# Two graph layers on one core: a block's projections dealt out between tiles of sums, and the second layer's sums zeroed by a product

## The chip, the cores and the metric

The kernel runs on one core of a Trainium2 chip. The metric is the device time of one execution in microseconds, as a median of repeated runs; lower is better. The engines are named as the profile names them: PE multiplies matrices (PEld loads its stationary operand), DVE is the vector engine, ACT the scalar engine, POOL issues the gathers and SP issues most other transfers.

## What is computed

There are N = 6250 nodes with D = 256 features, E = 100000 edges sorted by their target, and R = 8 kinds of edges. The input is normalised, goes through two graph layers, is added to the input, is normalised again, and goes through a mixture of 8 experts that picks 2 for each node. The two layers are this, cut to what matters:

```python
def _rgcn_conv(x, W, Wroot, b, src, dst, etype):
    xs = x[src]
    seg = dst * R + etype
    sums = segment_sum(xs, seg, num_segments=N * R)
    cnt = segment_sum(ones, seg, num_segments=N * R)
    mean = (sums / maximum(cnt, 1.0)[:, None]).reshape(N, R, -1)
    return x @ Wroot + b + einsum('nrd,rde->ne', mean, W)

h = relu(_rgcn_conv(layernorm(x), W1, Wroot1, b1, src, dst, etype))
h = _rgcn_conv(h, W2, Wroot2, b2, src, dst, etype)
x = x + h
x = x + moe(layernorm(x))
```

The targets are denser at low node numbers, so the first blocks of nodes have many more edges than the last.

## The kernel before, in words

**Preparation** (up to the first gather, at 83.5 us) normalises x, writes it to memory as three bfloat16 pieces (`xs[0]`), and works out where each tile of edges lands.

**A layer** is `layer(k)`, k = 0 and 1. The edges are 782 tiles of 128. A *group* is 1 to 6 neighbouring tiles; there are 194 groups, and `seq` is their order, which takes groups from the front (few nodes, many edges) and from the end (many nodes, few edges) in turn. One pass of the loop over `q` is a *step* and serves one group.

- `tiles_in(g)` takes one of two accumulators `pg` (PSUM, one bank of 2 KB for each of the 2 halves of the features, and a third in the first layer for the counts), has ACT fill it with zeros (L672), and for each tile has POOL gather 128 source rows into one of 13 buffers `ge` (L680) and DVE make the 0/1 matrix `oh` (L686). It is called one step ahead.
- `sums(g)` multiplies: 6 products on PE for each tile (L696; 3 pieces by 2 halves), and in the first layer a seventh with ones for the counts (L699). They accumulate in `pg`. The last product that reads a `ge` buffer sets that buffer free for a later gather.
- `add(g)` has DVE add `pg` to a ring in SBUF (L710). There are two rings, one for each end of the nodes; each holds RB = 3 blocks of 128 nodes.

**A block** is 128 nodes; there are 49. `whole[b]` is the step after which no edge of block b is left. The block's work is then due at fixed steps after it:

- `counts` and `invert` bring the counts to the partitions (first layer only);
- `project` (two steps on) multiplies the block's sums by the weights: 18 products in fp32 (2 halves for the root and 8 relations), each executed as two passes on PE, 36 passes in all (L783). They are made in five *pairs* of relations through a small PSUM tile `pr` with two buffers, and DVE adds each relation into `h` (L791, L793);
- `clear` (two steps on) has ACT zero the block's place in the ring (L800), after the projections have read it;
- `finish` (two steps on) writes the block's result: the three pieces of the next layer's input, or the output and its normalisation;
- `turn` (three steps on) transposes it, and `logits` (four on) makes the expert scores in the second layer.

The step in the loop, in order: `tiles_in` of the next group, `project` and `clear`, `turn`, `finish`, `sums`, `invert` and `logits`, `add`, then `root`, `counts` and `join`. This is the order of the program. A scheduler in the compiler's front end then orders each engine's instructions by that and by when it takes their operands to be ready, so products of `project` and of `sums` can already be mixed on PE. [...]

**Bounds.** `_plan` also works out which part of a ring a group may touch at each step (`bounds`, checked at run time), so that an `add` need not wait for the projections that read other blocks. READ is the number of steps after `whole[b]` at which no add may touch block b any more, TAKE = 3 the number after which the block's cleared place may be used again.

**After the layers** 53 tiles of 256 chosen rows go through the experts (L1186 to L1230).

Of the kernel before, what the change touches and what calls it, by code (L numbers as in the profile page):

```python
# [39 lines left out]
BF16 = mybir.dt.bfloat16  # L40
# [8 lines left out]
P = 128  # L49
# [45 lines left out]
Z = 4.8  # L95
WIN = 64
RB = 3
READ = 2
TAKE = 3
EARLY = 30  # L100

# [1 line left out]
def _plan(N, E, R):  # L103

    T = -(-E // P)

    def windows(ts, n):

        mid = n // 2
        lo, hi = [0] * n, [-(1 << 30)] * n
        for t in ts:
            for k in range(n + 1):
                i0, i1 = t * P, max(0, t + k - mid) * P
                mean = N * (i1 * i1 - i0 * i0) / (E * E)
                sd = 2 * N * i0 / (E * E) * math.sqrt(abs(i1 - i0)) + 0.004 * abs(mean)
                if k < n:
                    lo[k] = min(lo[k] if t != ts[0] else 1 << 30, math.floor(mean - Z * sd) - (k < mid))
                if k:  # L120
                    hi[k - 1] = max(hi[k - 1], math.ceil(mean + Z * sd) + (1 if k <= mid else 2))
        shift = -min(lo)
        w = [(a + shift, b + shift) for a, b in zip(lo, hi)]
        return shift, w, max(b for _, b in w)


    NB = -(-N // P)
    mid = max(0, round((N / 4 - P / 2) / P))
    split = round(T * math.sqrt((mid + 0.5) * P / N))
    regions = []  # L130
    t = 0
    while t < T:
        left = (split if t < split else T) - t
        for n in range(min(6, left), 0, -1):
            ng = max(1, min(36, left) // n)
            shift, w, width = windows((t + n // 2, t + n * (ng - 1) + n // 2), n)
            if width <= WIN:
                break
        regions.append((t, n, ng, shift, w, width))
        t += n * ng  # L140
    groups = []
    for r, (t0, n, ng, *_) in enumerate(regions):
        for g in range(ng):
            groups.append((t0 + g * n, n, r))
    NG = len(groups)
    up = [g for g in range(NG) if groups[g][0] < split]
    down = list(range(NG - 1, len(up) - 1, -1))
    size = [sum(groups[g][1] for g in s) for s in (up, down)]
    seq, at, n = [], [0, 0], [0, 0]
    while len(seq) < NG:  # L150

        s = int(n[1] * (size[0] - EARLY) < n[0] * size[1])
        if at[s] == len((up, down)[s]):
            s = 1 - s
        g = (up, down)[s][at[s]]
        seq.append(g)
        at[s] += 1
        n[s] += groups[g][1]
    step = {g: q for q, g in enumerate(seq)}

    whole = []
    for b in range(NB):
        if b == mid:
            whole.append(NG - 1)
            continue
        p = math.sqrt((b + 1 if b < mid else b) * P / N)
        dev = Z * math.sqrt(E * p * (1 - p)) + 1
        t = int(min(E - 1, E * p + dev) // P) if b < mid else int((E * p - dev) // P)
        whole.append(step[next(g for g, (t0, n, _) in enumerate(groups) if t0 + n > t)])


    bounds = []
    for g in range(NG):
        read, taken = ([b for b in range(NB) if whole[b] + n < step[g]] for n in (READ - 1, TAKE))
        if g < len(up):
            bounds.append((sum(b < mid for b in read) or -NB, sum(b < mid for b in taken) + RB))
        else:
            n = sum(b > mid for b in read)
            bounds.append((NB - sum(b > mid for b in taken) - RB, NB - n if n else 2 * NB))
    return T, regions, groups, seq, len(up), mid, whole, bounds  # L180
# [3 lines left out]
def kernel(  # L184
# [20 lines left out]
    nc = tc.nc  # L205
    N, D = x.shape
    E = src.shape[0]
# [428 lines left out]
    with tc.If(go == 1) as cmp:  # L636
        with ExitStack() as arm:
# [4 lines left out]
            hTs = ap.tile([P, NB, KD, P], F32, name="hTs", bufs=1)  # L642
            zeros = ap.tile([P, WIN], F32, name="zeros", bufs=1)
            nc.vector.memset(zeros, 0.0)
            rings = [ap.tile([P, KD + 1, R, RING + WIN], F32, name=f"ring{i}", bufs=1) for i in range(2)]

            step = {g: q for q, g in enumerate(seq)}
# [8 lines left out]
            def layer(k):  # L656
# [11 lines left out]
                def tiles_in(g):  # L668
                    t0, n, r = groups[g]
                    pg = psum.tile([P, nd, R, WIN], F32, name="pg", tag="pg", bufs=2)  # L670
                    wd = regions[r][5]
                    state["zeroed"] = nc.scalar.copy(pg[:, :nd, :, :wd],  # L672
                                                     zeros[:, None, None, :wd].to_broadcast([P, nd, R, wd]))
                    got = []
                    ohs = ap.tile([P, OHW], BF16, name="oh", bufs=3)
                    o0 = 0
                    for t in range(t0, t0 + n):
                        m = P if t < EC else ER
                        ge = ap.tile([P, 3, KD, P], BF16, name="ge", bufs=13)
                        nc.gpsimd.indirect_dma_start(  # L680
                            out=ge[:m].rearrange("p s k d -> p (s k d)"), out_offset=None, in_=xs[k][:, :],
                            in_offset=bass.IndirectOffsetOnAxis(ap=idx[:m, t : t + 1], axis=0))
                        a, b = regions[r][4][t - t0]
                        oh = ohs[:m, o0 : o0 + (b - a) * R].rearrange("p (r d) -> p r d", r=R)
                        o0 += (b - a) * R
                        nc.vector.tensor_scalar(oh, iota16[:m].rearrange("p (r d) -> p r d", r=R)[:, :, a:b],  # L686
                                                rel[:m, t : t + 1], None, op0=OP.is_equal)
                        got.append((ge, oh, m, a, b))
                    state[g] = (pg, got)

                def sums(g):
                    pg, got = state[g]
                    for ge, oh, m, a, b in got:
                        for c in range(KD):
                            for s in range(3):
                                nc.tensor.matmul(pg[:, c, :, a:b], ge[:m, s, c, :], oh, start=False, stop=False,  # L696
                                                 skip_group_check=True)
                        if nd > KD:
                            nc.tensor.matmul(pg[:, KD, :, a:b], ones16[:m], oh, start=False, stop=False,  # L699
                                             skip_group_check=True)  # L700

                def add(g):
                    pg, _ = state.pop(g)
# [59 lines left out]
                def invert(b):  # L763
                    if k == 0:
# [2 lines left out]
                        nc.vector.tensor_scalar(invs[:, b], pc[:, :R], 1.0, None, op0=OP.max)  # L767
                        nc.vector.reciprocal(invs[:, b], invs[:, b])

                def project(b):  # L770

                    n = rows(b)
# [3 lines left out]
                    h = ap.tile([P, D], F32, name="h", bufs=2)  # L776
                    lhs = [(R, [xT[:, c, :n] for c in range(KD)])]
                    lhs += [(r, [ring[:, c, r, s0 : s0 + n] for c in range(KD)]) for r in range(R)]
                    for i in range(0, R + 1, 2):
                        pr = psum.tile([P, 2, D], F32, name="pr", tag="mm", bufs=MM)  # L780
                        for j, (r, chunks) in enumerate(lhs[i : i + 2]):
                            for c in range(KD):
# [5 lines left out]
                        for j, (r, _) in enumerate(lhs[i : i + 2]):  # L788
                            if r == R:
                                extra = bias1 if k == 0 else state.pop(("xb", b))  # L790
                                nc.vector.tensor_tensor(h[:n], pr[:n, j], extra[:n], OP.add)  # L791
                            else:
                                nc.vector.scalar_tensor_tensor(h[:n], pr[:n, j], invs[:n, b, r : r + 1], h[:n],  # L793
                                                               op0=OP.mult, op1=OP.add)
                    state["h", b] = h

                def clear(b):
# [47 lines left out]
                tiles_in(seq[0])  # L845
                due = {}
                for b, q in enumerate(whole):
                    for d, f in ((-1, root), (0, counts), (1, invert), (2, project), (2, clear), (2, finish), (3, turn), (4, logits)):
                        due.setdefault(q + d, []).append((f, b))

                todo = []
# [8 lines left out]
                def run(q, *fs):  # L860
                    for f, b in due.get(q, []):
                        if f in fs:
                            f(b)

                cleared[:] = [[(-1, ins) for _, ins in c] for c in cleared]
                for q in range(NG + 5):
                    if k == 1 and q == 2:

                        with tc.issue_after(state["zeroed"].ins):
# [4 lines left out]
                    if q == 0 and k == 0:  # L874
                        for c in range(KD + 1):
                            nc.vector.memset(rings[0][:, c], 0.0)
                            nc.scalar.copy(rings[1][:, c], zeros[:, None, 0:1].to_broadcast([P, R, RING + WIN]))
                    run(q, project, clear)
                    run(q, turn)
                    run(q, finish)  # L880
                    if q < NG:
                        sums(seq[q])
                    run(q, invert, logits)
                    if q < NG:
                        add(seq[q])
# [388 lines left out]
```

## Time and profile before

| | us |
|---|---|
| median of 7 runs | 3022.39 |
| lowest, highest | 3014.03, 3025.11 |
| the profiled execution | 3029.28 |
| its span (first to last instruction) | 3027.4 |
| first gather of the first layer, last gather | 83.5, 1124.9 |
| first gather of the second layer, last gather | 1163.3, 2161.4 |
| PE, DVE, ACT, POOL busy in the span | 2562.7, 1622.0, 1019.4, 1808.6 |

The span holds the preparation, the two layers and the experts one after the other, so a share of the whole span is an average over parts that differ; each part is read by itself. A group of instructions is a line with its engine, operation and tiles; behind its busy time stand the idle time of the engine just before them and what ended it. "issue" is time for which the profile shows no cause. A busy PE counts the modelled ends of pipelined products, so the distance from one start to the next is the better price of a product in a row of them.

### The profile page before, as it was taken

Reading aid. Unit: us, or ns where it says so; the run is one execution under the profiler, and the core shown is the slowest. Engines: PE = TensorE matmul, PEld = TensorE weight load, DVE = VectorE, ACT = ScalarE, POOL = GpSimd, SP = SyncE. Lnnn points to the kernel's source line nnn. Section 1 sums busy time; section 2 is a strip of 40 time slices with the busy share of each in tenths; the row PEclk is TensorE's granted clock in tenths of the full one; section 3 lists DMA queues with packets and bytes.
Section 4 is the critical chain, followed back from the end, with each engine's and each line's share of the span. In section 5 each row is a group of like instructions: output and inputs, shape, how many; then the busy total and the mean of one; then the engine's idle time right before and its main releaser. Section 6 shows DMA issues by size and latency. Waiting matters only on the chain.

```text
span 3027.4 us, 52037 instructions
## 1 busy us (share of the span) xinstructions
PE 2562.7 (85%) x18131; PEld 2165.1 (72%) x18131; DVE 1622.0 (54%) x4676; ACT 1019.4 (34%) x1378; POOL 1808.6 (60%) x2109
## 2 busy tenths in 40 slices
PE   5578887888888886887888888898839999999997
PEld 2467676776777775766766776777728888888886
DVE  7567676767676674666766776676711111111111
ACT  6334443434343442332323323233312222222221
POOL 1667776777777764777777777777413333333332
PEclk9788998989998997989989998999969999999998
DMA  7555555555555554666566666666363444444441
GB/s 250 156 150 162 170 166 155 172 162 170 163 172 159 167 148 132 179 178 172 168 175 176 172 178 170 175 179 174 108 201 116 112 114 107 108 121 107 107 123 18
DMA packets 215592, 461.05 MB, mean 152 GB/s; under 512 B 50717, under 2 KB 123223, under 8 KB 215191
## 3 DMA queue, kind: packets, MB, share of 16 engines
q0 software_dynamic: 120384, 334.45, 40.8%
q1 hardware_dynamic: 83724, 112.33, 11.0%
q10 hardware_dynamic: 11210, 10.81, 1.1%
q8 instruction: 149, 2.44, 0.3%
q14 instruction: 125, 1.02, 0.1%
HBM read 412.02 MB, written 46.31 MB: 151 GB/s over the span
## 4 chain that ended last, share of the span: by engine, by line
PE 64%; DMA 19%; DVE 5%; ACT 5%; issue 4%; POOL 1%; SPq 0%; DVEq 0%; ACTq 0%; POOLq 0%
PE pr L783 25%; DMA ge<-xs,idx 14%; PE ph L1214 12%; PE po L1225 12%; PE pg L696 11%; ACT ring L800 2%; DVE ring L710 2%; ACT pg L672 2%; DMA cn<-ring 1%; POOL ge L680 1%; DMA xt<-in_x_dram 1%; PE pg L699 1%; PE pt L1198 1%; DVE h L793 1%; DMA fw<-in_L_ffn_W_dram 1%
## 5 line engine op out<-in xcount | busy, mean ns | idle before, releaser
L680 POOL DMA_INDIRECT ge<-xs,idx x1564 | 1519.4, 971 | 625.6 <-issue 224.8
L696 PE MATMUL pg<-oh,ge 128*128 128x200 bf16 (+24 forms) x9384 | 835.3, 242 | 313.8 <-DMA ge<-xs,idx 216.4
L696 PEld LDWEIGHTS <-ge 128*128 128x128 bf16 x9384 | 675.9, 105 | 436.3 <-DMA ge<-xs,idx 270.5
L783 PE MATMUL pr<-gw,ring 128*128 128x256 f32 (+1 forms) x3136 | 754.8, 396 | 2.3 <-DVE h L793 1.6
L783 PEld LDWEIGHTS pr<-gw,ring 128*128 128x128 f32 (+1 forms) x3136 | 617.0, 200 | 100.0 <-DVE h L793 5.8
L710 DVE TENSOR_TENSOR ring<-pg,ring 128x1176 f32 (+31 forms) x388 | 456.4, 1176 | 278.6 <-PE pg L696 136.1
L672 ACT COPY pg<-zeros 128x1176 f32<-128x1176 f32 (+31 forms) x388 | 380.2, 981 | 537.7 <-DVE ring L710 512.1
L793 DVE SCALAR_TENSOR_TENSOR h<-pr,invs,h 128x256 f32<-128x256 f32 (+1 forms) x784 | 376.3, 480 | 163.3 <-PE pr L783 146.5
L800 ACT COPY ring<-zeros 128x3072 f32<-128x3072 f32 (+1 forms) x98 | 227.8, 2324 | 682.9 <-PE pr L783 623.5
L1215 ACT ACTIVATE hT<-ph,bcol 128x256 f32<-128x256 f32 x424 | 200.8, 474 | 535.1 <-PE ph L1214 535.1
L1214 PE MATMUL ph<-xT,w 128*128 128x256 f32 x1696 | 377.9, 381 | 0.0
L1225 PE MATMUL po<-fw,hT 128*128 x1696 | 374.4, 379 | 0.0
L1225 PEld LDWEIGHTS po<-fw,hT 128*128 128x128 f32 x1696 | 322.2, 190 | 43.8
L1214 PEld LDWEIGHTS ph<-xT,w 128*128 128x128 f32 x1696 | 320.8, 192 | 42.1
L686 DVE TENSOR_SCALAR oh<-iota,rel 128x152 bf16<-128x152 f16 (+25 forms) x1564 | 337.3, 275 | 16.1 <-PE pg L699 14.1
L1186 POOL DMA_INDIRECT xg<-xnd,ti x106 | 105.4, 995 | 347.6 <-DMA ti<-tlist 256.3
L1230 POOL DMA_INDIRECT out_dram<-fo,ti x106 | 168.8, 1593 | 233.5 <-DVE wt L1199 126.9
L1228 DVE TENSOR_TENSOR fo<-po,b2b 128x256 f32<-128x256 f32 x106 | 45.0, 424 | 299.3 <-PE po L1225 299.3
L699 PE MATMUL pg<-oh,ones 128*128 128x128 bf16 (+24 forms) x782 | 189.2, 242 | 0.0
L1209 DVE COPY bcol<-b1c 128x8 f32 x53 | 9.0, 172 | 302.4 <-ACT hT L1215 301.9
L699 PEld LDWEIGHTS <-ones 128*128 128x128 bf16 x782 | 83.1, 106 | 2.7
L783 PE MATMUL pr<-gw,tT 128*128 128x256 f32 (+1 forms) x196 | 70.1, 490 | 2.3 <-ACT tT L316 1.4
(190 smaller groups left out, 1347.4 us busy)
## 6 DMA issues: line engine op xcount, KB each, us to landing
w<-in_L_ffn_W_dram SPq DMA_DIRECT2D x53, 1024.0 KB
ge<-xs,idx POOLq DMA_INDIRECT x1564
xt<-in_x_dram SPq DMA_DIRECT2D x96, 128.0 KB
xs<-xb SPq DMA_DIRECT2D x8, 1152.0 KB
xs<-hb SPq DMA_DIRECT2D x48, 192.0 KB
fw<-in_L_ffn_W_dram ACTq DMA_DIRECT2D x8, 1024.0 KB
xt<-in_x_dram SPq DMA_DIRECT2D x8, 768.0 KB
out_dram<-h SPq DMA_DIRECT2D x48, 128.0 KB
```

What stands on the lines that cost most here:

```text
L672: state["zeroed"] = nc.scalar.copy(pg[:, :nd, :, :wd], zeros[:, None, None, :wd].to_broadcast([P, nd, R, wd]))
L680: nc.gpsimd.indirect_dma_start(out=ge[:m].rearrange("p s k d -> p (s k d)"), out_offset=None, in_=xs[k][:, :], in_offset=bass.IndirectOffs ...
L686: nc.vector.tensor_scalar(oh, iota16[:m].rearrange("p (r d) -> p r d", r=R)[:, :, a:b], rel[:m, t : t + 1], None, op0=OP.is_equal)
L696: nc.tensor.matmul(pg[:, c, :, a:b], ge[:m, s, c, :], oh, start=False, stop=False, skip_group_check=True)
L699: nc.tensor.matmul(pg[:, KD, :, a:b], ones16[:m], oh, start=False, stop=False, skip_group_check=True)
L710: a = nc.vector.tensor_tensor(slot, pg[:, :nd, :, :wd], slot, OP.add).ins
L783: mm = nc.tensor.matmul(pr[:n, j], chunks[c], w[:, c, r, :], start=(c == 0), stop=(c == KD - 1))
L793: nc.vector.scalar_tensor_tensor(h[:n], pr[:n, j], invs[:n, b, r : r + 1], h[:n], op0=OP.mult, op1=OP.add)
L800: ins = nc.scalar.copy(at, zeros[:, None, None, 0:1].to_broadcast([P, nd, R, P]))
L1214: nc.tensor.matmul(ph[:, :TK], w1[:, k, h * P : (h + 1) * P], xT[:, k, :], start=(k == 0), stop=(k == KD - 1))
L1215: nc.scalar.activation(hT[:, h, :], ph[:, :TK], AF.Gelu, bias=bcol[:, h : h + 1], scale=1.0)
L1225: nc.tensor.matmul(po[:, :D], hT[:, k, f * P : (f + 1) * P], rhs, start=(k == 0), stop=(k == KH - 1))
```

## The change

Three things are changed in `layer`, and one in `_plan`.

1. `project` no longer makes its five pairs at once. It puts them in a list, `pairs`. `sums` takes one from the list after each tile (`go_on`), and what is left when the group has no more tiles is made then.
2. `project` is called just ahead of `sums`, after `turn`, `clear` and `finish`. `clear` and `finish` are due three steps after `whole[b]` in place of two, `turn` four in place of three, `logits` five in place of four, and the loop runs one step longer.
3. In the second layer, from step 3 on, `tiles_in` has no copy of zeros on ACT. `sums` begins with one product of a matrix of ones with a tile of bfloat16 zeros for each of the two banks, started afresh (`start=True`), and the sums accumulate on it. The first layer, and the first three groups of the second, keep the copy.
4. `_plan` takes READ as 1 in effect (a block that is whole may be touched by no later step's add), and in exchange takes a tile's uncertainty of place as P / 4 edges in place of 1. With these sizes `whole` differs for two of the 49 blocks, by one step each.

The product for the counts also writes one row in place of 128 equal ones.

```diff
-        dev = Z * math.sqrt(E * p * (1 - p)) + 1
+        dev = Z * math.sqrt(E * p * (1 - p)) + P / 4
...
-        read, taken = ([b for b in range(NB) if whole[b] + n < step[g]] for n in (READ - 1, TAKE))
+        read, taken = ([b for b in range(NB) if whole[b] + n < step[g]] for n in (0, TAKE))
...
+            zeros16 = ap.tile([P, R * WIN], BF16, name="zeros16", bufs=1)
+            nc.vector.memset(zeros16, 0.0)
...
-                    state["zeroed"] = nc.scalar.copy(pg[:, :nd, :, :wd],
-                                                     zeros[:, None, None, :wd].to_broadcast([P, nd, R, wd]))
+                    if k == 0 or step[g] < 3:
+                        state["zeroed"] = nc.scalar.copy(pg[:, :nd, :, :wd],
+                                                         zeros[:, None, None, :wd].to_broadcast([P, nd, R, wd]))
...
                     pg, got = state[g]
+                    wd = regions[groups[g][2]][5]
+                    for c in range(nd if k and step[g] >= 3 else 0):
+                        nc.tensor.matmul(pg[:, c, :, :wd], ones16, zeros16[:, : R * wd].rearrange("p (r d) -> p r d", r=R),
+                                         start=True, stop=False, skip_group_check=True)
...
                         if nd > KD:
-                            nc.tensor.matmul(pg[:, KD, :, a:b], ones16[:m], oh, start=False, stop=False,
+                            nc.tensor.matmul(pg[0:1, KD, :, a:b], ones16[:m, 0:1], oh, start=False, stop=False,
                                              skip_group_check=True)
+                        go_on()
...
+                pairs = []
+
+                def go_on():
+
+                    if pairs:
+                        f, i = pairs.pop(0)
+                        f(i)
...
-                    for i in range(0, R + 1, 2):
+                    def pair(i):
                         pr = psum.tile([P, 2, D], F32, name="pr", tag="mm", bufs=MM)
...
+                    pairs.extend((pair, i) for i in range(0, R + 1, 2))
                     state["h", b] = h
...
-                    for d, f in ((-1, root), (0, counts), (1, invert), (2, project), (2, clear), (2, finish), (3, turn), (4, logits)):
+                    for d, f in ((-1, root), (0, counts), (1, invert), (2, project), (3, clear), (3, finish), (4, turn), (5, logits)):
...
-                for q in range(NG + 5):
+                for q in range(NG + 6):
...
-                    run(q, project, clear)
-                    run(q, turn)
+                    run(q, turn, clear)
                     run(q, finish)
+                    run(q, project)
                     if q < NG:
                         sums(seq[q])
+                    while pairs:
+                        go_on()
                     run(q, invert, logits)
```

More of the change, by code (lines that the diff above doesn't have):

```diff
@@ L97 @@
 RB = 3
-READ = 2
 TAKE = 3
```

## The prediction, made before the changed kernel was run

> **What bounds the kernel now.** First the table by stage, over five stretches cut at the first and last gather of each layer (time, busy time of PE, PEld, DVE, ACT and POOL with instructions, granted clock, DMA share and GB/s).
>
> ```profile
> 83.50:1124.90 1041.40, 863.97 (x7333) 740.16 (x7334) 704.12 (x1660) 437.03 (x476) 766.10 (x781) 0.91 0.57 163
> 1124.90:1163.30 38.40, 25.97 (x156) 21.43 (x154) 21.57 (x50) 12.74 (x17) 0.98 (x2) 0.89 0.13 41
> 1163.30:2161.40 998.10, 834.17 (x6713) 690.69 (x6714) 668.40 (x2176) 301.86 (x363) 751.38 (x781) 0.91 0.61 175
> 2161.40:2265.00 103.60, 48.84 (x257) 37.87 (x256) 38.27 (x160) 19.21 (x28) 8.50 (x9) 0.72 0.45 149
> 2265.00:3027.40 762.40, 744.39 (x3546) 655.16 (x3544) 134.80 (x410) 196.35 (x414) 266.71 (x204) 0.99 0.40 104
> ```
>
> PE looks like the bound with 83% in both layers, but it is idle 177 and 164 us there. POOL's busy time hides something: the timeline of POOL (start, duration, idle before and its cause) shows that it has no rest between gathers that it could use.
>
> ```profile
> 949.64 0.95 POOL L680 DMA_INDIRECT ge<-xs,idx  x1 [0.30 <-PE pg L699]
> 950.89 0.95 POOL L680 DMA_INDIRECT ge<-xs,idx  x1 [0.30 <-issue]
> 952.14 0.95 POOL L680 DMA_INDIRECT ge<-xs,idx  x1 [0.30 <-issue]
> 958.51 0.94 POOL L680 DMA_INDIRECT ge<-xs,idx  x1 [5.42 <-PE pg L696]
> 959.76 0.95 POOL L680 DMA_INDIRECT ge<-xs,idx  x1 [0.30 <-issue]
> ```
>
> A gather takes 0.95 and a gap of 0.30 follows whatever is named behind it: a pitch of 1.25 us. A layer has 782 gathers, so 781 pitches, 976 us at least. The layers take 1041.4 and 998.2 from first to last gather. Read gather by gather, 40 distances in the first layer and 23 in the second are 1.4 us or more; beyond 1.25 each they hold 62.7 and 18.9 us. The short ones average 1.253. So the layers are bound by POOL's pitch, and at most 82 us of stalls can be won: time that POOL loses is not made up.
>
> What makes the stall at 952? The timeline of PE in the same place:
>
> ```profile
> 951.57 0.23 PE L696 MATMUL pg<-oh,ge 128*128 128x152 bf16 x1
> 951.64 6.25 PE L783 MATMUL pr<-gw,ring 128*128 128x256 f32 x28
> 957.73 0.51 PE L696 MATMUL pg<-oh,ge 128*128 128x152 bf16 x5
> ```
>
> The 36 passes of a block's projection run in a row (8 us, 28 of them here) and no sum frees a buffer; the 13 buffers run out and POOL stands still until the first tile after it. Of the stalls, 16 in the first layer have over 2 us of projection in the 4 us before them or within; they hold 39.0 us. The 24 others hold 23.7. In the second layer it is 11 with 11.2 and 12 with 7.8. The chain of waits agrees that L783 is where PE's time is on the path, but its share, 25%, overstates it: a projection that POOL overlaps costs nothing.
>
> ```profile
> PE 64%; DMA 19%; DVE 5%; ACT 5%; issue 4%; POOL 1%; SPq 0%; DVEq 0%; ACTq 0%; POOLq 0%
> ```
>
> **The change part by part.**
>
> *Dealing, first layer.* What counts is the order on PE, which the scheduler makes. In the built order of before, 26 of the 49 blocks have their 36 passes with no more than one product of sums between them; in that of the changed kernel 9. Of these 2 at the end have no sums left beside them in either, so 24 lumps become 7. The others already had sums between, because the scheduler mixes; for the first dozen blocks the two orders are nearly the same, and 6.3 us of the 39.0 (three stalls at 178 to 205) lie there and stay. Of the other 32.7 I take the share of lumps that go, 17 of 24: 23 us. Bounds: 0 (what is dealt only stalls in smaller pieces) and 39. That a dealt pair fits: a pair is 8 passes at 216 ns, 1.7 us, and a tile's seven products about 0.5, so five tiles take 11 us in which POOL issues 8.8: PE falls 3.8 tiles back, where a lump of 8 us puts it 6.2 back. What is late next is the landing of a gather, which PE waits for 85.1 us in this layer already, and then POOL's pitch.
>
> *Dealing, second layer.* 20 lumps, 3 of them at the end, become 6 with the same 3: 17 become 3. 11.2 us by 14/17 is 9 us. Bounds 0 and 11.2.
>
> *The product with zeros.* 191 groups by 2 products, 382, of 395 columns on average (8 times the group's width). The nearest rows are products of sums: 200 columns start 90 ns apart, 256 columns 116, so 0.45 ns a column and 178 ns each: 68 us of PE. From above: the product of 512 columns at L521 takes 405 ns alone, 155 us if none is pipelined. PE's idle 164 us in this layer hides either; what hides it is POOL's pitch, and without that cover it would be the 68 us in full. It goes out of a reserve, though: 834 busy becomes 902 of 998, and PE catches up more slowly after a projection. Removed are as many copies of 0.82 us on ACT (158 us), off the path: ACT is busy 302 of 998. PE waited for that copy 16.0 us in all in this layer, and now PE itself waits for the `add` two groups back, a shorter chain; behind that wait stand the sums of the group and the pair dealt into it. I take +4 us for the two together, between −8 (half of the 16.0 ends stalls) and +25 (the rival below). In the first layer the copy stays, and so do the 71.6 us that PE waits for it.
>
> *Steps moved.* `clear` goes on ACT one step later, so an `add` that waits for it has less room, and behind that `add` on DVE stand the one-hots of the next tiles and the projections' additions. Before, DVE's `add` waited 5.2 us for L800 in the first layer. By the built orders the sums between a block's last pass and that `add` are 6 tiles or more for most blocks in both kernels, and 3 or fewer for some ten early ones in both. I take +2, between 0 and +10. `finish`, `turn` and `logits` a step later move their transfers too: SP's write of the pieces or the output and ACT's copies. Within a layer nobody waits for them; after the last group the steps hold nothing but these, so the 38.4 and the 103.6 us stay, ±3. Two blocks whole a step later, the memset of zeros (once, under 1 us on DVE) and the count's one row (782 products with the same columns, 242 ns each): 0.
>
> Sum: −23 − 9 + 4 + 2 = −26 us. The profiled execution took 3029.3, with 1.9 outside its span, so its like would take 3003. It lies 6.9 us above the median of the runs; the median goes from 3022.4 to 2996.
>
> [...] The layers ran at a mean granted clock of 0.91, the experts, where PE has no rests, at 0.99. [...]
>
> **The rivals.**
>
> *PE becomes the bound in the second layer; slower.* It decides from the point where PE needs over 976 us there, that is 142 us more than 834, or 0.37 us for each product with zeros. For it: 0.405 us is a row of this trace, if an isolated one, and each product with zeros can wait for DVE with the whole of PE behind it. Then PE needs 834 + 155 = 989 with no slack for its waits for gathers; if a quarter of the 131.3 us that it waits for them now comes on top, 1022, or 24 slower than 998, and with a gain of 10 to 20 kept in the first layer the kernel is 5 to 15 us slower, 25 to 30 if that fails. Against: sums in a row keep to 0.45 ns a column.
>
> *Nothing moves.* The scheduler mixes anyway, and the stalls are an effect of the bursts after a projection, in which POOL is behind, not of the lump: 24 and 12 stalls have no projection near. Then ±6 us.
>
> *All stalls go.* With shorter bursts the others vanish as well: 40 to 75 us, at 2947 to 2982. Against: many of the others come about every 57 gathers and hold about 1 us each in both layers, with PE in plain sums.
>
> That the change isn't what runs, because a bound is broken at run time and the kernel's other arm is taken, I exclude: worked out from the inputs, every bound holds in both kernels.
>
> **How the numbers follow.** Forecast, −12 to −45: 0.57. All stalls go: 0.10. Nothing moves: 0.13. Slower, mostly by 8 to 30: 0.20. A measurement here tells 0.2%, 6 us, from no change. Faster 0.67, same 0.13, slower 0.20. The range goes from 2962 (60 us) to 3035 (+13, which takes in the lower half of the slower case); the likeliest case's own range is 2977 to 3010.
>
> **What would show it.** In the profile after: the first layer's gathers should span 1005 to 1025 us and the second's 985 to 995; the long distances with projection near them should hold some 16 and 2 us, and the others stay at 24 and 8. PE in the second layer should rise by some 65 us, ACT fall by 158. I am wrong if POOL's stalls stay with PE's lumps gone, if the second layer lengthens with PE's idle near nothing, or if DVE's wait for the cleared ring grows past 10 us.

## The result, and the profile after

| | before | changed |
|---|---|---|
| median, us | 3022.99 (39 runs) | 3045.50 (15 runs) |
| lowest, highest | 3006.09, 3031.03 | 3034.96, 3052.80 |
| the profiled execution, its span | 3029.28, 3027.4 | 3049.69, 3047.9 |

The ratio, with its 95% interval, is 1.0078 [1.0068, 1.0089]: the changed kernel is 22.5 us slower by the medians, where 26 faster was forecast. In some of the runs below, on four chips, every kernel took a fifth to a quarter longer (the kernel before 3791 to 3838 us), so each kernel is compared only with the kernel before that was measured beside it.

In the changed kernel the gather is L682, the sums L702, the count's product L705, the product with zeros L697, the `add` L717, the projections L798, and the copy of zeros L674. The table by stage of the changed kernel, cut at the first and last gather of each layer (time; busy time of PE, PEld, DVE, ACT, POOL; granted clock, DMA share, GB/s):

```profile
83.90:1145.40 1061.50, 964.51 (x7324) 718.90 (x7325) 702.22 (x1656) 437.24 (x476) 763.06 (x781) 0.93 0.56 160
1145.40:1186.20 40.80, 31.65 (x164) 24.46 (x164) 23.02 (x53) 12.84 (x17) 0.96 (x2) 0.90 0.12 39
1186.20:2177.40 991.20, 871.83 (x7107) 702.46 (x7108) 665.51 (x2172) 148.75 (x173) 752.08 (x781) 0.94 0.62 176
2177.40:3047.90 870.50, 795.91 (x3789) 695.72 (x3787) 173.98 (x574) 215.19 (x441) 275.18 (x213) 0.95 0.41 109
```

The second layer did what was forecast: 991.2 us in place of 998.1. What follows its last gather takes 870.5 in place of 866.0, the stretch between the layers 2 more. The loss is in the first layer, 1061.5 in place of 1041.4, and there PE has nearly the same number of records (7324, before 7333) and is busy 100 us longer. Read gather by gather, POOL's stalls beyond 1.25 us grow from 62.7 to 82.4; those with a projection near them from 39.0 (16 stalls) to 59.7 (33), while the others hold 22.7 (before 23.7). That is one of the forecast's signs of being wrong: the lumps, blocks whose 36 passes have no more than one product of sums between them, fell in the traces from 26 to 9, as forecast from the built orders, and the stalls stayed.

Where do the 100 us come from? The timeline of PE in the changed kernel (start, duration, engine, line, operation, shape of the stationary operand, shape of the result, count):

```profile
956.63 0.23 PE L705 MATMUL pg<-oh,ones 128*1 128x136 bf16 x1
956.79 0.59 PE L702 MATMUL pg<-oh,ge 128*128 128x160 bf16 x6
957.30 0.23 PE L705 MATMUL pg<-oh,ones 128*1 128x160 bf16 x1
957.47 0.44 PE L846 MATMUL pt<-ident,h 128*128 128x128 f32 x2
```

and the same sequence in the kernel before:

```profile
959.64 0.23 PE L699 MATMUL pg<-oh,ones 128*128 128x136 bf16 x1
959.70 0.58 PE L696 MATMUL pg<-oh,ge 128*128 128x160 bf16 x6
960.12 0.23 PE L699 MATMUL pg<-oh,ones 128*128 128x160 bf16 x1
960.19 0.38 PE L830 MATMUL pt<-ident,h 128*128 128x128 f32 x2
```

The durations (second column) are equal; the starts are not. A tile's seven products, from 956.79 to 957.47, take 0.68 us, before 0.49. Over the whole layer, at full granted clock, the median from the last sum's start to the count's is 164 ns (before 69), and from there to the next sum 160 (before 70). That is 185 ns a tile, 145 us for 782 tiles if each ran at full clock and none waited. The groups show it from another side: PEld's idle ahead of the count's product (behind the second bar: idle time, then what ended it) was 2.7 us before,

```profile
L699 PEld LDWEIGHTS <-ones 128*128 128x128 bf16 x782 | 83.1, 106 | 2.7
```

and is 105.5 in the changed kernel, over half of it with no cause that the profile shows:

```profile
L705 PEld LDWEIGHTS <-ones 128*1 128x1 bf16 x782 | 61.9, 79 | 105.5 <-issue 57.9
```

### The profile page after: what moved, and what is told of

Read it like the earlier page. It is cut to its first block, busy times and chain, and to the rows that moved or that the text cites. A ratio compares the mean times of both kernels' runs of the same rounds, so it can differ in the third digit from the quotient of the medians.

```text
span 3047.9 us, 52499 instructions
## 1 busy us (share of the span) xinstructions
PE 2709.1 (89%) x18513; PEld 2161.1 (71%) x18513; DVE 1619.7 (53%) x4677; ACT 866.2 (28%) x1187; POOL 1806.3 (59%) x2110
## 5 line engine op out<-in xcount | busy, mean ns | idle before, releaser
L682 POOL DMA_INDIRECT ge<-xs,idx x1564 | 1517.1, 970 | 643.7 <-PE pg L702 220.2
L702 PE MATMUL pg<-oh,ge 128*128 128x200 bf16 (+24 forms) x9384 | 885.7, 238 | 206.0 <-DMA ge<-xs,idx 143.7
L702 PEld LDWEIGHTS <-ge 128*128 128x128 bf16 x9384 | 649.0, 103 | 376.5 <-DMA ge<-xs,idx 177.2
L798 PE MATMUL pr<-gw,ring 128*128 128x256 f32 (+1 forms) x3136 | 770.1, 392 | 3.0 <-DVE h L808 2.9
L798 PEld LDWEIGHTS pr<-gw,ring 128*128 128x128 f32 (+1 forms) x3136 | 590.0, 195 | 91.1 <-DVE h L808 5.9
L717 DVE TENSOR_TENSOR ring<-pg,ring 128x1464 f32 (+30 forms) x388 | 456.5, 1177 | 262.9 <-PE pg L702 119.1
L688 DVE TENSOR_SCALAR oh<-iota,rel 128x152 bf16<-128x152 f16 (+25 forms) x1564 | 331.2, 273 | 22.6 <-PE pg L705 18.8
L674 ACT COPY pg<-zeros 128x1176 f32<-128x1176 f32 (+17 forms) x197 | 223.1, 1135 | 415.4 <-DVE ring L717 401.6
L1204 POOL DMA_INDIRECT xg<-xnd,ti x106 | 105.5, 995 | 355.2 <-DMA ti<-tlist 229.5
L705 PE MATMUL pg<-oh,ones 128*1 128x128 bf16 (+24 forms) x782 | 180.1, 230 | 0.0
L705 PEld LDWEIGHTS <-ones 128*1 128x1 bf16 x782 | 61.9, 79 | 105.5 <-issue 57.9
L697 PE MATMUL pg<-zeros,ones 128*128 128x488 bf16 (+15 forms) x382 | 105.1, 355 | 2.1 <-DVE ring L717 1.8
```

Of the source, the lines that this page charges most:

```text
L674: state["zeroed"] = nc.scalar.copy(pg[:, :nd, :, :wd], zeros[:, None, None, :wd].to_broadcast([P, nd, R, wd]))
L682: nc.gpsimd.indirect_dma_start(out=ge[:m].rearrange("p s k d -> p (s k d)"), out_offset=None, in_=xs[k][:, :], in_offset=bass.IndirectOffs ...
L705: nc.tensor.matmul(pg[0:1, KD, :, a:b], ones16[:m, 0:1], oh, start=False, stop=False, skip_group_check=True)
L717: a = nc.vector.tensor_tensor(slot, pg[:, :nd, :, :wd], slot, OP.add).ins
L798: mm = nc.tensor.matmul(pr[:n, j], chunks[c], w[:, c, r, :], start=(c == 0), stop=(c == KD - 1))
```

## The experiments

Two theories stood against each other. **The count's one row**: a product whose stationary operand is narrow, among full ones, starts 95 ns later than a full one, and the product after it 90 ns later. PE then needs 965 us in the first layer, close to POOL's 976, and no longer catches up after a projection; dealing itself gains. The expectations call this the drain; that PE drains there was the author's assumption, and no run shows it: the late starts are what was measured (164 in place of 69 ns into the product, 160 in place of 70 out of it). **The rest of the change**: dealing in smaller pieces, the product with zeros or the moved steps lose by themselves, and the row is only what PE has time for.

**The first runs: the kernel before at 3791 to 3838.** *Wide* is the changed kernel with the count's product as it was; *narrow* the kernel before with the one-row product alone (the same lines, exchanged):

```diff
-  nc.tensor.matmul(pg[0:1, KD, :, a:b], ones16[:m, 0:1], oh, ...)
+  nc.tensor.matmul(pg[:, KD, :, a:b], ones16[:m], oh, ...)
```

*Narrow, grouped* makes the one-row products of a group in a row, behind all its sums. The output is the same:

```diff
   for ge, oh, m, a, b in got:
       ...   # 6 sums
-      if nd > KD: <one-row product>
+  for ge, oh, m, a, b in got:
+      if nd > KD: <one-row product>
```

*Dealing alone* is wide, with ACT's copy of zeros in both layers and no product with zeros:

```diff
-  if k == 0 or step[g] < 3:
+  if True:
       state["zeroed"] = nc.scalar.copy(...)
...
-  for c in range(nd if k and step[g] >= 3 else 0):
+  for c in range(0):
```

Wide:

> The changed kernel with the product for the counts 128 rows wide again, as before; all else of the change kept. Theory (the one-row product drains PE when it starts and when it ends, about 95 ns each time, 782 times two, 148 us of PE in the first layer): starts around the count's product fall from 166 to 70 ns apart, the first layer falls from 1061.6 to 1010 to 1025 us, the kernel to 2995 to 3010. Rival (the dealt order and the steps moved by one are what slowed the first layer): the first layer stays at 1050 to 1062 and the kernel at 3035 to 3046.

Narrow:

> The kernel before with nothing changed but the product for the counts, which writes one row in place of 128. Theory (drain): PE busy in the first layer rises by some 100 us, and as the projections still run in lumps the layer goes from 1041 to 1070 to 1095 us; the kernel is 30 to 55 us slower than before. Rival (the dealt order): no change, within 6 us.

Narrow, grouped:

> The kernel before with the one-row product, but all of a group's count products made in a row after the group's other products. If the cost is one of changing the shape on PE, it is paid 194 times two in place of 782 times two, 37 us of PE in place of 148, and the kernel is 5 to 15 us slower than before. If each one-row product is slow by itself, it is as slow as with the one-row product after each tile.

Dealing alone:

> The changed kernel with the wide product for the counts and with the copy of zeros on ACT in both layers: the dealing and the moved steps alone. The first layer should be as in the run with the wide product alone (1010 to 1025 us if the drain was the cause). The second layer tells who won its 7 us: 985 to 992 if the dealing did, 995 to 1000 if the product with zeros did.

| kernel | us | the kernel before beside it | ratio |
|---|---|---|---|
| wide | 3701.5 | 3834.3 | 0.9645 [0.9621, 0.9670] |
| narrow | 3832.9 | 3834.3 | 0.9997 [0.9979, 1.0015] |
| narrow, grouped | 3848.7 | 3834.3 | 1.0034 [1.0014, 1.0053] |
| dealing alone | 3699.6 | 3834.3 | 0.9650 [0.9622, 0.9679] |

None of these fits either theory as it stood: the gain of dealing was 3.5% and the one row's loss could not be measured. Wide and narrow again, and then the changed kernel itself:

> The changed kernel with the product for the counts 128 rows wide again, once more, since in the first comparison every kernel, that of before too, ran at some 3700 to 3850 us, with PE's signals reaching the other engines some 2.5 us late. Where the kernel before takes 3023 again: by the drain theory the first layer falls from 1061.6 to 1010 to 1025 us and the kernel to 2995 to 3010; by the rival (the dealt order and the moved steps) it stays at 3035 to 3046.

> The kernel before with nothing changed but the product for the counts, which writes one row in place of 128, once more for the same reason. Where the kernel before takes 3023 again: by the drain theory 30 to 55 us slower than before, by the rival no change.

> The changed kernel itself, on the same chip and at the same time as the kernel before, because in the comparisons so far the kernel before took 3830 us. If that lasts, the wide product for the counts alone gave 0.967 of the kernel before, and the changed kernel should lie above it by what the drain costs there: by the drain theory at 0.975 to 1.00, by the rival (the dealt order costs) at 0.967. If the kernel before takes 3023 again, 1.008.

Wide 3702.8 (0.9669 [0.9646, 0.9691]), narrow 3833.1 (1.0006 [0.9981, 1.0032]), and the changed kernel 3681.8 beside 3791.4: 0.9721 [0.9695, 0.9747], between what the two theories gave (0.975 to 1.00 and 0.967). So here the change as a whole was faster by 2.8%, and the sign of the result hangs on the conditions. The timelines show part of what differs. Narrow of the second time ("remote": the profile finds no instruction that released it): two products on PE, and the DVE and ACT instructions that wait for them.

```profile
1147.76 0.27 PE L766 MATMUL pc<-ident,cn 8*128 8x8 f32 x1
...
1147.96 0.69 PE L314 MATMUL pt<-ident,xt 128*128 128x128 f32 x2
...
1152.32 0.17 DVE L767 TENSOR_SCALAR invs<-pc 128x8 f32<-128x8 f32 x1 [5.69 <-remote]
...
1152.41 0.37 ACT L316 COPY tT<-pt 128x256 f32<-128x256 f32 x1 [7.04 <-remote]
```

The pair with DVE in the trace of before:

```profile
759.51 0.22 PE L766 MATMUL pc<-ident,cn 8*128 8x8 f32 x1 [0.45 <-DMA cn<-ring]
...
759.77 0.17 DVE L767 TENSOR_SCALAR invs<-pc 128x8 f32<-128x8 f32 x1 [0.49 <-PE pc L766]
```

In the first, DVE and ACT both stand idle for some 4 us after PE's products are recorded as ended (1148.03 and 1148.65), and go on within 0.1 us of each other; PE itself has its next product at 1152.84. In the second DVE starts 0.04 us after the end. In 19 of the 49 blocks of narrow's second run DVE was idle for over 1 us in this way, in the trace of before in none; in its first run 15 waits of DVE ahead of L767 that ended "remote" hold 48.2 us, the longest 5.7 (from 75 to 1550 us of its span). The 2.5 us in the expectation of wide's second run are the author's estimate. From the first gather to the last, stretches of over 0.8 us in which PE (weight loads too), DVE and ACT all rest are 113 with 297 us there, before 42 with 57. A gather takes 0.95 us in both, DVE and ACT are as busy as before, and the part with the experts is nearly as long (874 us after the last gather, before 866). PE's products do take longer: narrow has PE busy 2938.0 us here and 2674.8 in the run below with the kernel before at 3025, at a mean granted clock of 0.843 and 0.927. Together the rests and PE's longer work are well short of the 790 us between these two executions, so where the rest of the time goes, what brings the hold-ups, whether the low clock is their cause or their effect, and why the loss of the one row does not show here, all stay open.

**How narrow is narrow?** The kernel before with its count's product written to 64 and to 96 equal rows in place of 128, one execution each:

```diff
-  nc.tensor.matmul(pg[:, KD, :, a:b], ones16[:m], oh, ...)
+  nc.tensor.matmul(pg[0:W, KD, :, a:b], ones16[:m, 0:W], oh, ...)    # W = 64, 96
```

> The kernel before with the product for the counts writing 64 rows in place of 128. One look, for the distance from start to start around that product. If what drains PE is the change between the array as a whole and a part of it, 64 columns are such a part: about 95 ns more into the product and out of it, as with one column. If it is something of the single column or row, 70 ns as before.

> The same with 96 rows. [...] If any width under 128 drains, 165 ns.

With 64 the starts are 164 ns (into the product) and 186 (out of it) apart; with 96 both are 69, as with 128. So a slower load of the weights isn't what delays the starts: in the median one load takes 127 ns with 96 columns, 106 with 64, 101 with 128 and 79 with one. Their times, 3800.4 and 3791.0 beside 3791.4, tell nothing under these conditions; the distances do.

**Wide, with the kernel before at 3021.**

> The changed kernel with the wide product for the counts, an hour later. If the kernel before takes some 3023 us again: by the drain theory a first layer of 1010 to 1025 us and 2995 to 3010 in all, by the rival (dealt order and moved steps) 1050 to 1062 and 3035 to 3046. If the kernel before still takes some 3800: 0.965 of it, as twice before.

3009.48 beside 3020.89, 0.9953 [0.9937, 0.9969]. One line put back takes the kernel from 22.5 us slower to 11.4 faster; its first layer is 2 us over the range that the theory of the one row gave. Its stages (first layer, second layer, rest):

```profile
83.50:1110.20 1026.70, 851.02 (x7328) 730.97 (x7329) 698.39 (x1657) 433.42 (x476) 762.96 (x781) 0.92 0.57 166
1149.80:2141.70 991.90, 868.98 (x7106) 700.93 (x7107) 665.51 (x2172) 148.66 (x173) 753.45 (x781) 0.94 0.62 176
2141.70:3011.20 869.50, 792.75 (x3790) 693.26 (x3788) 173.89 (x574) 215.21 (x441) 275.13 (x213) 0.95 0.40 109
```

PE's 964.5 us in the first layer are 851.0 again and the layer is 35 us shorter; the second layer and the rest are as in the changed kernel.

**The parts, one by one; the kernel before at 3025.1.** Narrow:

> The kernel before with nothing changed but the product for the counts, one row in place of 128, now that the kernel before takes some 3021 us again. In the changed kernel the wide product is worth 34 us (3045.5 to 3009.5 by the medians). If the drain's price is the same without dealing, 25 to 45 us slower than before; with the projections in lumps it may be more, up to 55. If the price exists only beside the dealing, within 6 us of before.

3060.90, 1.0117 [1.0098, 1.0137]: 36 us slower with nothing dealt, as the theory has it. Its first layer:

```profile
83.50:1154.80 1071.30, 972.99 (x7332) 727.55 (x7333) 706.57 (x1660) 440.46 (x476) 763.12 (x781) 0.92 0.56 159
```

PE is busy 109 us more, and the layer is 30 us longer: the stalls near projections go from 39.0 us to 75.3, the others from 23.7 to 17.7. The chain of waits has PE at 69% in place of 64, and the count's product at 3% in place of 1.

Dealing alone:

> The dealing and the moved steps alone: wide product for the counts, copy of zeros on ACT in both layers. The run with the product with zeros gave 3009.5, a first layer of 1026.8 and a second of 991.9. First layer 1027 again. If the product with zeros costs the 4 us that the prediction gave it, 3004 to 3007; if it helps the second layer, that layer is 993 to 998 here and the kernel 3011 to 3016.

3014.69, 0.9965 [0.9952, 0.9978]. Neither case came as stated: the kernel lies in the second range, but its second layer, 990.7 us, is as short as with the product with zeros. The two layers:

```profile
83.50:1112.30 1028.80, 851.47 (x7316) 729.73 (x7317) 697.11 (x1656) 433.52 (x476) 763.63 (x782) 0.92 0.58 165
1155.10:2145.80 990.70, 827.62 (x6720) 683.46 (x6721) 663.67 (x2170) 298.19 (x364) 749.20 (x781) 0.91 0.63 176
```

The product with zeros alone: the kernel before with the copy left out from step 3 of the second layer, and the two products in `sums` (the diff of the change, point 3).

> The kernel before with the product with zeros in the second layer and nothing else. First layer as before, 1041. Second: 998 plus 4 by the prediction's step, between 990 (the shorter chain ends stalls) and 1023 (PE becomes the bound). From start to start a product with zeros of 395 columns should take 0.17 to 0.18 us.

3030.98, 1.0020 [1.0007, 1.0034]: 6 us slower; its second layer has 1008.8 us. Its first layer, in which PE executes the same products in the same order as in the kernel before, has 1037.9 us in place of 1041.4: so far apart are two executions of the same thing. From start to start a product with zeros takes 182 ns in the median at full granted clock.

The moved steps alone, with the bounds of `_plan` as changed: dealing alone, but with the pairs made at once where `project` stands.

```diff
-  pairs.extend((pair, i) for i in range(0, R + 1, 2))
+  for i in range(0, R + 1, 2): pair(i)
```

> The changed kernel's steps without the dealing: clear, finish, turn and logits a step later, the five pairs made at once as before, the wide product for the counts, the copy of zeros on ACT. The prediction gave the moved steps +2 us. If they are what kept the first layer from the forecast 1018, it is 1045 to 1050 here and the kernel 5 to 12 us slower than before; if not, 1041 and no change. The stretch after the last gather, 3.5 us longer in the changed kernel than in that of before, is longer here too if the moved steps are its cause.

3028.37, 1.0011 [0.9997, 1.0024]. The two layers and the rest:

```profile
81.90:1122.70 1040.80, 852.82 (x7320) 735.22 (x7321) 701.67 (x1659) 435.16 (x476) 763.33 (x782) 0.92 0.58 163
1162.50:2164.00 1001.50, 839.16 (x6723) 701.60 (x6724) 666.61 (x2171) 298.48 (x364) 754.29 (x781) 0.89 0.62 174
2164.00:3033.40 869.40, 793.96 (x3790) 694.02 (x3789) 174.33 (x577) 214.73 (x441) 274.97 (x213) 0.95 0.42 109
```

The first layer is as before, so the moved steps didn't slow it; the rest is 3.4 us longer, in the changed kernel 4.5.

**Narrow, grouped, again.** If it is the switch of shape and not the one row, products in a row should pay it once a group. In the first of these two runs the kernel before took 3838, in the second 3021.

> The kernel before with the one-row product, a group's count products in a row after its other products, now that the kernel before takes some 3021 us again. The one-row product after each tile cost 36 us. If the cost is that of changing the shape, 194 times two changes in place of 782 times two leave a quarter of it, 9 us (0 to 15). If each one-row product is slow by itself, 36 again.

> The kernel before with the one-row product, a group's count products in a row after its other products; a third time, for a time in which the kernel before takes some 3021 us. By the change of shape 0 to 15 us slower than before; if each one-row product is slow by itself, 36.

3841.95 beside 3837.88 (1.0017 [0.9998, 1.0036]); then 3036.39 beside 3020.90, 1.0063 [1.0046, 1.0080]. The first layer of the second, nearly (its gathers run from 82.2 to 1129.4, 1047.2 us):

```profile
83.50:1131.00 1047.50, 888.34 (x7324) 719.61 (x7325) 702.44 (x1656) 436.15 (x475) 763.50 (x781) 0.91 0.57 162
```

Narrow products behind one another start 63 ns apart, and PE's extra is 24 us in place of 109: the switch is what costs PE its time. The kernel's time is 15 us over the kernel before by the medians, 14 to 24 by the interval, and not the 9 that a quarter of 36 would be; its first layer is 6 us longer in this execution, and where the remainder arises was not located.

**The product with zeros in both layers**, which takes ACT's copy out of the first layer too (wide, `if step[g] < 3:` for the copy, and its opposite for the products):

> A version that might beat both: the changed kernel with the wide product for the counts and with products with zeros in both layers, three a group in the first. The wide product alone gave 3009.5. In the first layer PE waits 71.6 us for the copies on ACT in the kernel before, and 191 times 3 products of some 0.17 us, 100 us of PE, take their place: PE at some 960 of 1027 us busy. If the waits matter more, the first layer falls to 1010 to 1020 and the kernel to 2995 to 3005; if PE's reserve does, 1030 to 1060 and 3015 to 3040.

> Products with zeros in both layers with the dealing and the wide product for the counts, once more for the same reason. While every kernel was slow it took 0.961 of the kernel before, against 0.965 and 0.967 of the wide product alone. If PE's wait for the copies matters more than its reserve: 2995 to 3005; if the reserve does: 3015 to 3040.

3683.95 beside 3837.88 (0.9610 [0.9583, 0.9637]); then 3007.75 beside 3020.90, 0.9956 [0.9938, 0.9973]. In the second its first layer shows

```profile
83.50:1101.00 1017.50, 905.75 (x7894) 756.81 (x7904) 699.07 (x1656) 228.41 (x285) 766.43 (x781) 0.96 0.58 167
```

From first to last gather it has 1018.6 us, 8 less than wide in this one execution, at ACT's 228 in place of 433; the time of the runs is that of wide within the intervals, and above the 2995 to 3005 of the hopeful case. Wide, dealing alone and this one beat both the kernel before and the changed one.

## Why the prediction was wrong, point by point

**The step that failed** is the last in "Steps moved": "the count's one row (782 products with the same columns, 242 ns each): 0". It measured 36 us alone (3060.9 against 3025.1) and 34 in the changed kernel (22.5 slower against 11.4 faster for wide; 38 by the ratios). The error was to price it by its duration, when a product's price in a row is the distance between starts: the durations before and after, 242 and 230 ns, still say nothing. And the trace of before did hold the row. The group

```profile
L411 PE MATMUL rpl<-rcol,rnum 128*8 128x128 bf16 x98 | 18.8, 228 | 9.1 <-DVE rcol L410 6.1 <-DVE rids L416 2.7
```

has a stationary operand of 8 columns. Where full products of L696 stand before or behind it, its starts lie 180 and 152 ns apart from theirs; where it follows itself, 56. By that, against 69 and 70, an estimate for 782 products is (111 + 82) ns × 782 = 151 us of PE at full clock, from 864 to 1015, over POOL's 976: the rival "PE becomes the bound", in the other layer and by another edit. Measured were 100 us more in the changed kernel and 109 alone, to 965 and 973, just under 976.

That the loss is 36 and not 109 fits the reserve that was counted on: PE was idle 177 us in the first layer. The stalls show where that reserve was at work: alone, the row adds 36 us to those near projections, where PE has to catch up with POOL, and nothing to the others.

With that step set right the forecast is still off: wide is 11.4 us faster, where the other terms gave 26. What is missing is mostly the dealing.

The distances say which widths pay: products with 64, 8 and 1 stationary columns start late (164, 180 and 164 ns into them, in place of 69), one with 96 does not (69). That the change of shape makes PE wait is argued from these distances and from the products in a row, 63 ns apart; by what mechanism, no run shows.

**Dealing in the first layer**, forecast −23: half right. Against the moved steps alone, 1040.8 to 1028.8 is −12. The late stalls went as argued: beyond the first 260 gathers those near projections hold 32.0 us before, 25.2 in the run with the product with zeros alone (whose first layer is that of before) and 26.6 with the moved steps, but 15.1 with dealing and 13.3 in wide, where 10 was forecast. The early ones, of which 6.3 were to stay, did not: 6.9 before, 16.3 with the moved steps alone, 13.6 with dealing, 15.1 in wide. But they hold 12.4 in the run with the product with zeros alone too, so one execution differs from the next by much of that growth, and what the change adds to it isn't settled.

One thing that lengthened is PE's wait for the copy of zeros, over the whole layer: 71.6 us before and 75.0 in the other execution of the same layer, 87.9 with the moved steps, 95.1 with dealing alone, 92.4 in wide. "In the first layer the copy stays, and so do the 71.6 us" missed this for the wide kernels; in the changed kernel, with PE itself slower, it is 57.4. Such a wait in the changed kernel's timeline of PE, a stretch of dealt passes and what follows it:

```profile
489.74 2.86 PE L798 MATMUL pr<-gw,ring 128*128 128x256 f32 x12
495.01 0.56 PE L702 MATMUL pg<-oh,ge 128*128 128x80 bf16 x6 [2.42 <-ACT pg L674]
```

and of POOL in the same place, where the gather stands still until those sums have run:

```profile
488.45 0.94 POOL L682 DMA_INDIRECT ge<-xs,idx  x1 [0.30 <-issue]
495.84 0.94 POOL L682 DMA_INDIRECT ge<-xs,idx  x1 [6.45 <-PE pg L702]
```

With the copy gone there too, the early stalls near projections hold 3.7 us, but the late ones 18.9; PE is busy 906 us there in place of wide's 851. That its longer work gives back what the copy cost is likely and was not tested.

**Dealing in the second layer**, forecast −9: right. 998.1 to 990.7 against the kernel before is −7, 1001.5 to 990.7 against the moved steps −11. Other executions agree: without dealing and with the copies this layer takes 998.1 to 1003.0 us in four kernels, with dealing 989.6 to 991.9 in four. Its stalls near projections fall from 11.2 to 5.5, where 2 was forecast. The profiles' sum for both layers against the moved steps is −23 in one execution each; the medians, 3028.4 and 3014.7, give −14 of the 32 forecast. The share of lumps that go was the wrong measure for the first layer: the lumps went as counted, and half of the gain came.

**The product with zeros**, forecast +4 at 68 us of PE: right in size, and the cover held. Alone it costs 6 us; beside dealing it costs nothing that can be told (0.9953 and 0.9965, with intervals that overlap). PE's busy time rose by 38 in the second layer and ACT's fell by 153, forecast 65 and 158. From start to start a product with zeros takes 183 ns in the median at full granted clock, where 178 was forecast. Its group in the changed kernel has PE idle before it for hardly anything, so the wait for the `add` two groups back came to nothing:

```profile
L697 PE MATMUL pg<-zeros,ones 128*128 128x488 bf16 (+15 forms) x382 | 105.1, 355 | 2.1 <-DVE ring L717 1.8
```

**The moved steps**, forecast +2: +3, with an interval that takes in no change. DVE's wait for the cleared ring is 5.2 us in the first layer before and after, so that worry was empty. What it costs lies elsewhere: behind the last gather there are 869.4 to 872.1 us in the five kernels with the moved steps, 861.5 to 866.0 in the four without; forecast was ±3.

**The clock**: dealing did not lower it. The layers' granted clock went from 0.91 and 0.91 to 0.93 and 0.94 in the changed kernel, and with PE no busier than before it was 0.92 and 0.91 in dealing alone.

## What to carry to other kernels

Price an instruction on a pipelined engine by the distance between starts in the mix in which it will stand, and search the trace for the nearest row of the new *shape*, not only of the same size of work: an operand that is cut to what is needed can be dearer than a full one (here 3060.9 us against 3025.1). Count every edit as a suspect, the one-line tidying too; here it outweighed all the others. And an engine that is idle a sixth of the time is not free when it has to catch up after bursts: of the 109 us that the one row added to PE alone, 30 to 36 reached the end.

## What the runs showed of the hardware

- On PE a product with 1, 8 or 64 stationary columns between products with 128 starts late: from start to start 164 to 180 ns in place of 69 into it, and 152 to 186 in place of 70 out of it (medians at full granted clock). With 96 columns there is no such delay (69 and 69), and products with one column behind one another start 63 ns apart.
- On four chips there were conditions in which the kernel before took 3791 to 3838 us in place of some 3023, and the verdict on the change turned round (0.972 in place of 1.008). In those traces DVE starts over 1 us after the recorded end of the product of PE that it waits for in 12 to 19 of 49 blocks, and in none of the others; gathers, DVE and ACT keep their durations, PE's products take longer at a lower granted clock (0.843 and 0.927 in two executions of narrow). These experiments met no chip in both conditions, and the cause stays open.
